# Windowed linear attention on one core: stores moved to ScalarE, halves of q and k stored twice and held in two buffers, masks of the scores in another order

## The chip, the core and the metric

The kernel runs on one core of a Trainium2 chip. A core has TensorE (PE in the profile; its weight loads are PEld), VectorE (DVE), ScalarE (ACT), GpSimd (POOL) and SyncE (SP), each with its own instruction queue that is worked off in order. Transfers (DMAs) are issued by an instruction on one of these queues and then run on 16 shared DMA engines. The metric is the device time of one execution in microseconds (us); the time of a version is the median of its runs.

## The reference

The input x is 4 x 256 x 48 x 48 in float32. Four layers each add to x a function of its group norm (32 groups): a 7 x 7 dilated convolution whose softmax weighs 49 shifted copies, a 3 x 3 convolution of signs, a 3 x 3 convolution with ternary weights, and the layer that the change touches, layer 3:

```python
q = sigmoid(einsum('bchw,oc->bohw', x, Wq)).reshape(b * 8, 32, 48, 48)   # k likewise
v = einsum('bchw,oc->bohw', x, Wv).reshape(b * 8, 32, 48, 48)
v = v / maximum(norm(v, axis=1), 1e-12)
Ik, Ikv = integral(k), integral(einsum('bfhw,bghw->bfghw', k, v))
for w in (1, 2, 4):
    ws = 48 // w
    wk, wkv = box(Ik, ws), box(Ikv, ws)          # sums over a ws x ws window, cut at the edges
    attn = einsum('bdhw,bdfhw->bfhw', q, wkv)
    norm = einsum('bdhw,bdhw->bhw', q, wk)
    outs.append(attn / (norm[:, None] + 1e-6))
x = x + einsum('bchw,oc->bohw', concatenate(outs, axis=1), Wout) + bout
```

`integral` and `box` are cumulative sums in both directions and their four-corner differences with edge padding, so a window of half width h (24, 12, 6) reaches the positions -h to h - 1 around a query as far as the image goes.

## The kernel before, in words

Layers 0 to 2 come first and are not changed. Layer 3 does not form the box sums of k v; it computes scores between keys and queries, masks them by each window, and multiplies them with v.

**Tiling.** The 48 x 48 positions are cut in 6 row blocks of 8 rows (`RB`); a row block has 384 positions (`NB`). A key tile is 8 rows by 16 columns, 128 positions, so there are 18 per image. The 8 heads are taken 4 at a time, which are the 128 channels of one channel block (`ct` or `mo`, 2 of them). A block of work (`Block`) is one batch, one channel block and one row block of queries: 48 blocks. A block meets the key tiles that its widest window sees, so the stream has 720 steps in all, each a pair of block and key tile.

**A step.** `scores` (called by `score`) multiplies, for a pair of heads (`pr` 0 or 1), a key tile with the queries into one of the two PSUM buffers `s`. Keys and queries are in float32r, split in a rounded half `hi` and a remainder `lo`; the contraction of 128 is four groups of 32, keys (hi, lo, hi, lo) against queries (hi, hi, lo, lo). `masked` (called by `cut`) then cuts the scores out of PSUM into a tile `sm`: where the key tile's rows lie wholly in the widest window, only the strips at its column edges are masked by VectorE (`widest`); the middle window is masked by VectorE (`middle`) or, in tiles two row blocks away, copied plainly by ScalarE (`copy`); a narrower window is masked by GpSimd from the middle one. Elsewhere VectorE masks the whole tile. Two steps later (`LAG`) `sums` multiplies `sm` with v into the accumulators `acc0` to `acc2`; what lies wholly in the widest window comes as one product of q with a summed state (`whole`). At a block's end the accumulators are copied to `stage`.

**Order of the work.** The program is written out by hand in one order, and every engine is kept to it: the helper `InOrder` (L149) records each instruction, which is why nearly every row of the profile carries L149 and tiles must tell the rows apart. In each turn of the main loop: fetch the keys of four steps on (`EARLY`), the scores and masks of the second pair of heads, the scores and masks of the next step's first pair, the sums of two steps ago, then one call of `advance`.

**Background.** `advance` lets a list of generators take one step each, as far as they are due; `yield n` means "again in n steps". `take` waits until a buffer counted in `free` is free, `bank` until the shared PSUM bank is, `wait_for` until something is in `made`; `until` turns `advance` inside the main loop until something is made. The generators are:
- `Projection` for the next batch: `load` of x, `qk` (a matmul into `proj_ps`, `sg` by sigmoid, for keys `kt` in the tiles' order, stores to `q_d`, `k_d`, `kf_d`, then `hi` by ScalarE, `lo` by GpSimd, and their stores to `kst_d` and `qst_d`) and `v`;
- `k_sums`: running sums of k (`cs`, a scan on VectorE), column sums of the three windows (`pt`, VectorE, then row by row on GpSimd), stored to `kb_d`;
- `norms`: loads `nhi`, `nlo`, `nq`, multiplies differences of `kb_d` with q on GpSimd, sums over channels on TensorE (`norm_ps`), stores `ns` to `n_d`, loads `nr`, takes its reciprocal, stores `r_d`;
- `state` and `window_state`: sums of k v for `whole`;
- `prepare` and `finish`: load the first channel block's result (`o`) and the norms (`rc`), divide, multiply with Wout (`out_ps`), add x (`res`), store the output.

Each key projection stores its halves in 8 DMAs (two halves, four heads of 32 partitions), each query projection in 8 likewise. `keys` has 7 slots (`KEYS`); a key tile is loaded into the slot whose content is needed latest, by two DMAs of 64 partitions, and a block's queries by four DMAs for each pair of heads. `hi`, `lo` and `pt` have one buffer each: the next writer waits until their stores have landed. In layer 3 all DMAs but two loads of constants are issued on SP's queue. Eight completion semaphores serve the DMAs of the hardware queues in turn, and each DMA waits for the one that used its semaphore before, eight issues back.

## Time and profile before

| | |
|---|---|
| time, 3 runs | 3889.24 us median (3881.86, 3889.24, 3891.01) |
| the profiled execution's own time | 3874.22 us |
| its span | 3872.4 us |
| TensorE matmuls | 3073.5 us, 79% of the span |
| VectorE | 2419.6 us, 62% |
| GpSimd | 1756.2 us, 45% |
| ScalarE | 723.8 us, 19% |
| mean granted TensorE clock | 0.911 |
| DMA | 624.08 MB; q1, which nearly all use, 53.3% of 16 engines |

The page gives the busy time of each engine, the span in 40 slices, the DMA queues, the chain that ended last, the costliest groups of instructions, and the DMA issues. A group is named by line, engine, operation and tiles (out<-in); `keys<-kst_d` is a load of `keys` from `kst_d`, `kst_d<-hi` a store of `hi`. The figures behind it are busy time, the mean of one instruction in ns, and the idle time just before such instructions with what ended most of it. "PE s <- DVE sm" among the waits says that TensorE's writes of `s` waited for VectorE's writes of `sm`, with the total in us, how often, and the longest. Instructions that issue DMAs are not counted as busy. The page's chain that ended last covers only a sliver of this span, so stretches and waits carry the reading here. Layer 3's scores run from 1431 us to the end; the projections that feed its first batch run before, beside the end of layer 2.

### The profile page before, as it was taken

What the parts mean: (1) busy time and instruction counts of PE and PEld (TensorE: products, weight loads), DVE (VectorE), ACT (ScalarE), POOL (GpSimd) and SP (SyncE); (2) the same over time, 40 slices, a digit from 0 to 9 for tenths busy, and PEclk for the clock granted to TensorE, in tenths of its full rate; (3) what the DMA queues carried; (4) which work ended last, traced back from release to release, by engine and by line L of the source; (5) the groups of instructions that cost most, each with busy time, mean ns of one, the idle gap of its engine ahead of it and who ended that gap; (6) DMA issues with size and microseconds to landing.
All of it is one profiled execution on the core that took longest, in us unless ns stands there. A gap on an engine that the chain in (4) does not pass through costs nothing. (4 is left out here: it accounts for less than half of the span.)

```text
span 3872.4 us, 70429 instructions
## 1 busy us (share of the span) xinstructions
PE 3073.5 (79%) x25874; PEld 2092.5 (54%) x25874; DVE 2419.6 (62%) x4987; ACT 723.8 (19%) x1652; POOL 1756.2 (45%) x2644
## 2 busy tenths in 40 slices
PE   3689998998996676577778767778877768989888
PEld 2567677777774464344445444445545445555554
DVE  7876685685653365566656556666556756667665
ACT  0012111111115322222111222211122211111110
POOL 0000210210201145667776567766667767665553
PEclk9799999999998888888889988889988889999999
DMA  7745233234235354566666557666756656754553
GB/s 247 239 134 179 79 122 114 85 120 124 79 100 160 113 145 148 169 196 186 181 176 200 175 177 208 195 185 188 205 166 192 202 161 199 198 149 137 164 145 106
DMA packets 529705, 624.08 MB, mean 161 GB/s; under 512 B 162867, under 2 KB 411475, under 8 KB 528339
## 3 DMA queue, kind: packets, MB, share of 16 engines
q1 hardware_dynamic: 528163, 617.79, 53.3%
q8 instruction: 209, 3.42, 0.4%
q0 software_dynamic: 144, 0.99, 0.1%
q14 instruction: 133, 1.09, 0.1%
q10 hardware_dynamic: 1056, 0.79, 0.1%
HBM read 451.32 MB, written 169.00 MB: 160 GB/s over the span
## 5 line engine op out<-in xcount | busy, mean ns | idle before, releaser
L149 DVE TENSOR_TENSOR sm<-s,masks 128x128 f32<-128x128 f32 (+8 forms) x2592 | 1129.6, 495 | 743.3 <-ACT sm L149 298.1
L149 POOL TENSOR_TENSOR sm<-sm,masks 128x432 f32<-128x432 f32 (+14 forms) x1152 | 825.0, 730 | 751.1 <-DVE sm L149 607.4
L149 PE MATMUL s<-qst,keys 128*128 128x320 f32 (+3 forms) x2880 | 781.2, 379 | 362.1 <-DVE sm L149 200.2
L149 PEld LDWEIGHTS s<-qst,keys 128*128 128x128 f32 x2880 | 477.8, 202 | 639.1 <-issue 310.2
L149 PE MATMUL acc<-sm,vs 128*32 128x64 f32 (+13 forms) x14976 | 697.7, 317 | 7.3 <-POOL sm L149 7.3
L149 PE MATMUL cv<-vx,wt 128*128 128x288 f32 x2080 | 559.1, 425 | 92.8 <-DVE vx L149 51.0
L149 PEld LDWEIGHTS cv<-vx,wt 128*128 128x128 f32 x2080 | 402.3, 198 | 213.4 <-issue 56.4
L149 PEld LDWEIGHTS acc<-sm,vs 128*32 128x32 f32 x14976 | 359.3, 114 | 256.6 <-issue 179.6
L149 ACT COPY sm<-s 128x234 f32<-128x234 f32 (+5 forms) x384 | 131.1, 341 | 1076.7 <-PE s L149 882.7
L149 POOL MEMSET v<- 128x16 f32 (+1 forms) x120 | 18.5, 215 | 684.0 <-DVE vx L149 629.3
L149 PE MATMUL cv<-v,wl 128*128 128x384 f32 x1152 | 228.4, 358 | 29.4 <-DVE x L149 10.8
L149 PEld LDWEIGHTS cv<-v,wl 128*128 128x128 f32 x1152 | 217.2, 197 | 40.9 <-issue 19.5
L149 DVE TENSOR_TENSOR pt<-cs 128x384 f32<-128x384 f32 x144 | 112.7, 784 | 150.1 <-DMA kb_d<-pt 140.6
L149 POOL TENSOR_TENSOR pt<-pt 128x144 f32<-128x144 f32 x336 | 182.9, 544 | 27.7 <-DVE pt L149 5.6
L149 POOL TENSOR_TENSOR v<-l2v,v 128x384 fp32r<-128x384 f32 x96 | 108.4, 1158 | 102.9 <-ACT v L149 93.9
L149 POOL TENSOR_TENSOR nhi<-nhi,nq 128x384 f32<-128x384 f32 x144 | 148.8, 1061 | 0.0
L149 PE MATMUL cv<-pad,wl 128*128 128x384 bf16 x864 | 143.1, 328 | 0.0
L149 PE MATMUL proj_ps<-wv_sb,xn 128*128 128x256 f32 x288 | 91.9, 450 | 59.8 <-ACT sg L149 40.5
L149 PE MATMUL out_ps<-o,wout_sb 128*128 128x384 f32 x288 | 126.3, 521 | 12.7 <-POOL o L149 7.6
L149 PE MATMUL proj_ps<-xn,wk_sb 128*128 128x384 f32 x192 | 89.2, 594 | 52.4 <-ACT vt L149 19.5
L149 PE MATMUL out_ps<-stage,wout_sb 128*128 128x384 f32 x288 | 120.0, 499 | 0.7 <-DVE stage L149 0.7
L149 PEld LDWEIGHTS <-wl 128*128 128x128 bf16 x864 | 83.8, 97 | 59.2 <-issue 0.6
(178 smaller groups left out, 3508.4 us busy)
## 6 DMA issues: line engine op xcount, KB each, us to landing
keys<-kst_d SPq DMA_DIRECT2D x960, 128.0 KB
wt<-wt SPq DMA_DIRECT2D x48, 768.0 KB
qst<-qst_d SPq DMA_DIRECT2D x384, 96.0 KB
kb_d<-pt SPq DMA_DIRECT2D x48, 576.0 KB
rc<-r_d SPq DMA_DIRECT2D x192, 144.0 KB
nhi<-kb_d SPq DMA_DIRECT2D x120, 192.0 KB
nlo<-kb_d SPq DMA_DIRECT2D x88, 192.0 KB
o_d<-stage SPq DMA_DIRECT2D x24, 576.0 KB
```

What stands on the lines that cost most here:

```text
L149: return lambda *args, **kwargs: self.tc.keep_in_program_order(op(*args, **kwargs))
```

## The change

- `kst_d` and `qst_d` hold each half twice, in the order of the contraction: a dimension of 4 in place of 2. A key tile is then loaded by one DMA of 128 partitions in place of two of 64, and a pair's queries by one in place of four.
- The halves are stored by DMAs from all 128 partitions: 12 for a key projection (four copies, three key tiles) in place of 8, and 4 for a query projection in place of 8.
- These stores, and those of `k_d`, `q_d`, `kf_d`, `n_d` and `o_d`, are issued on ScalarE's queue in place of SP's.
- `hi` and `lo` have two buffers in place of one, and they and `pt` are counted as free only 6 steps after their stores (`STORED`). What depends on them is marked as made before this hold.
- `KEYS` is 6 in place of 7, and a slot whose key tile the present step still uses is not taken (`used`, `idle`).
- `norms` issues all loads of `nhi` and `nq` for both channel blocks at once, and loads `nlo` piecewise, one window at a time, in two buffers, with a step after each piece.
- In `masked`, `middle` and `widest` come before `copy`.
- In the main loop the masks of the next step's first pair stand after `advance` in place of before the sums; their scores stay where they were.

```diff
--- before.py
+++ after.py
@@ -81,9 +81,10 @@
 NKT = NRB * NKC
 
 LAG = 2
-KEYS = 7
+KEYS = 6
 EARLY = 4
 QST = 4
+NLO = 2
 ATTN_EPS = 1e-6
 
 
@@ -226,11 +227,11 @@
     k_d = [dram.tile([C, HW], F32, tag=f"k{b}", name=f"k_d{b}") for b in range(B)]
     v_d = [dram.tile([P, NKT, HEADS, D], F32, tag=f"v{b}", name=f"v_d{b}") for b in range(B)]
     kst_d = [
-        dram.tile([NCT, NKT, 2, D, HEADS // NCT, P], F32, tag=f"kst{b}", name=f"kst_d{b}")
+        dram.tile([NCT, NKT, 4, D, HEADS // NCT, P], F32, tag=f"kst{b}", name=f"kst_d{b}")
         for b in range(B)
     ]
     qst_d = [
-        dram.tile([NCT, NRB, 2, D, HEADS // NCT, NB], F32, tag=f"qst{b}", name=f"qst_d{b}")
+        dram.tile([NCT, NRB, 4, D, HEADS // NCT, NB], F32, tag=f"qst{b}", name=f"qst_d{b}")
         for b in range(B)
     ]
     kf_d = [dram.tile([C, HW], F32, tag=f"kf{b}", name=f"kf_d{b}") for b in range(B)]
@@ -280,9 +281,10 @@
         bank_free = step + steps
 
 
-    free = {"xr": 2, "xn": 2, "kt": 2, "sq": 2, "vt": 1, "hl": 1, "ku": 1, "pt": 1, "cs": 1, "o": 1, "rc": 2, "res": 2}
+    free = {"xr": 2, "xn": 2, "kt": 2, "sq": 2, "vt": 1, "hl": 2, "ku": 1, "pt": 1, "cs": 1, "o": 1, "rc": 2, "res": 2}
 
     FETCH = 4
+    STORED = 6
 
     def take(what):
         while free[what] == 0:
@@ -379,30 +381,31 @@
                 act.copy(kt.rearrange("p (c r x) -> p c r x", c=NKC, x=KC), rows)
             yield 1
             if name == "k":
-                sync.dma_start(out=k_d[b][chans, cols], in_=kt)
-            sync.dma_start(out=(q_d if name == "q" else kf_d)[b][chans, cols], in_=t)
+                act.dma_start(out=k_d[b][chans, cols], in_=kt)
+            act.dma_start(out=(q_d if name == "q" else kf_d)[b][chans, cols], in_=t)
             yield from take("hl")
-            hi, lo = (self.scr.tile([P, NB], F32R, tag=x, name=x, bufs=1) for x in ("hi", "lo"))
+            hi, lo = (self.scr.tile([P, NB], F32R, tag=x, name=x) for x in ("hi", "lo"))
             whole = t if name == "q" else kt
             act.copy(hi, whole)
             yield 1
             pool.tensor_sub(lo, whole, hi.bitcast(F32))
             yield 2
-            for half, part in enumerate((hi, lo)):
-                for g in range(HEADS // NCT):
-                    src = part[g * D : (g + 1) * D].bitcast(F32)
-                    if name == "q":
-                        sync.dma_start(out=qst_d[b][mo, a, half, :, g, :], in_=src)
-                    else:
-                        sync.dma_start(
-                            out=kst_d[b][mo, a * NKC : (a + 1) * NKC, half, :, g, :].rearrange(
-                                "c d n -> d c n"
-                            ),
-                            in_=src.rearrange("p (c n) -> p c n", n=P),
+            for n in range(4):
+                if name == "q":
+                    act.dma_start(
+                        out=qst_d[b][mo, a, n].rearrange("d g n -> g d n"),
+                        in_=(hi, lo)[n // 2].bitcast(F32),
+                    )
+                else:
+                    for c in range(NKC):
+                        act.dma_start(
+                            out=kst_d[b][mo, a * NKC + c, n].rearrange("d g n -> g d n"),
+                            in_=(hi, lo)[n % 2][:, c * P : (c + 1) * P].bitcast(F32),
                         )
-            free["hl"] += 1
             free["kt"] += 1
             made.add((name, b, mo, a))
+            yield STORED
+            free["hl"] += 1
 
         def v(self, g, a, c):
             b = self.b
@@ -1607,8 +1610,9 @@
                 out=kb_d[b][:, chans, a * RB : (a + 1) * RB, :].rearrange("w p r x -> p w (r x)"),
                 in_=pt.rearrange("p w r x -> p w (r x)"),
             )
+            made.add(("kb", b, mo, a))
+            yield STORED
             free["pt"] += 1
-            made.add(("kb", b, mo, a))
 
         def norms(b, rb):
 
@@ -1618,7 +1622,6 @@
             def load(ct):
                 chans = slice(ct * P, (ct + 1) * P)
                 hi = scr.tile([P, NW, RB, W], F32, tag="nhi", name="nhi")
-                lo = scr.tile([P, NW, RB, W], F32, tag="nlo", name="nlo", bufs=1)
                 qf = scr.tile([P, RB, W], F32, tag="nq", name="nq")
                 sync.dma_start(
                     out=qf.rearrange("p r w -> p (r w)"),
@@ -1637,31 +1640,41 @@
                             out=hi[:, wi, n:RB],
                             in_=kb_d[b][wi, chans, H - 1 : H, :].to_broadcast([P, RB - n, W]),
                         )
-
-                    y0 = rb * RB - h - 1
-                    n = min(RB, max(0, -y0))
-                    if n < RB:
-                        sync.dma_start(
-                            out=lo[:, wi, n:RB], in_=kb_d[b][wi, chans, y0 + n : y0 + RB, :]
-                        )
-                return hi, lo, qf
+                return hi, qf
+
+            def load_lo(ct, wi):
+                y0 = rb * RB - HALVES[wi] - 1
+                n = min(RB, max(0, -y0))
+                if n == RB:
+                    return None, n
+                lo = scr.tile([P, RB, W], F32, tag="nlo", name="nlo", bufs=NLO)
+                sync.dma_start(
+                    out=lo[:, n:RB],
+                    in_=kb_d[b][wi, ct * P : (ct + 1) * P, y0 + n : y0 + RB, :],
+                )
+                return lo, n
 
             last = min(rb + HALVES[0] // RB, NRB - 1)
             yield from wait_for(
                 *((what, b, ct, at) for what, at in (("kb", last), ("q", rb)) for ct in range(NCT))
             )
-            for ct in range(NCT):
-                hi, lo, qf = load(ct)
-                yield FETCH
-                for wi, h in enumerate(HALVES):
-                    n = min(RB, max(0, h + 1 - rb * RB))
-                    if n < RB:
-                        pool.tensor_sub(hi[:, wi, n:RB], hi[:, wi, n:RB], lo[:, wi, n:RB])
+            loaded = [load(ct) for ct in range(NCT)]
+            pieces = [(ct, wi) for ct in range(NCT) for wi in reversed(range(NW))]
+            los = [load_lo(*pieces[n]) for n in range(NLO)]
+            yield FETCH
+            for at, (ct, wi) in enumerate(pieces):
+                hi, qf = loaded[ct]
+                lo, n = los.pop(0)
+                if lo is not None:
+                    pool.tensor_sub(hi[:, wi, n:RB], hi[:, wi, n:RB], lo[:, n:RB])
+                    if at + NLO < len(pieces):
+                        yield 1
+                if at + NLO < len(pieces):
+                    los.append(load_lo(*pieces[at + NLO]))
+                pool.tensor_mul(hi[:, wi], hi[:, wi], qf)
                 yield 1
-                for wi in range(NW):
-                    pool.tensor_mul(hi[:, wi], hi[:, wi], qf)
-                sums.append(hi)
-                yield 1
+                if wi == 0:
+                    sums.append(hi)
             yield 1
             yield from bank(1)
             ps = ps_m.tile([P, 512], F32, tag="st", name="norm_ps")
@@ -1679,7 +1692,7 @@
             act.copy(ns, ps[0 : D * NW, 0:NB])
             yield 1
             for wi in range(NW):
-                sync.dma_start(out=n_d[b][rb, :, wi, :], in_=ns[D * wi : D * wi + HEADS])
+                act.dma_start(out=n_d[b][rb, :, wi, :], in_=ns[D * wi : D * wi + HEADS])
             nn = HEADS * NW * NB // P
             nr = scr.tile([P, nn], F32, tag="nr", name="nr")
             flat = [d[b][rb].rearrange("h w n -> (h w n)") for d in (n_d, r_d)]
@@ -1765,11 +1778,12 @@
             stacks = []
             for pr in range(NPR):
                 st = qp.tile([P, 2, RB, W], F32, tag="qst", name="qst", bufs=QST)
-                for n in range(4):
-                    sync.dma_start(
-                        out=st[n * D : (n + 1) * D].rearrange("p j r w -> p j (r w)"),
-                        in_=qst_d[b][ct, rb, n // 2, :, 2 * pr : 2 * pr + 2, :],
-                    )
+                sync.dma_start(
+                    out=st.rearrange("p j r w -> p j (r w)"),
+                    in_=qst_d[b][ct, rb, :, :, 2 * pr : 2 * pr + 2, :].rearrange(
+                        "t d j n -> (t d) j n"
+                    ),
+                )
                 stacks.append(st.bitcast(F32R))
             return qs, stacks
 
@@ -1902,9 +1916,9 @@
 
 
 
-                copy(s, tiles)
                 middle(s, tiles)
                 widest(s, tiles)
+                copy(s, tiles)
 
                 wi = NW - 1 if many else 1
                 if wi in wis:
@@ -2009,7 +2023,7 @@
             b, ct, rb = order[i]
             yield 1
             if ct == 0:
-                sync.dma_start(out=o_d[b][rb], in_=stage.rearrange("p w n -> p (w n)"))
+                act.dma_start(out=o_d[b][rb], in_=stage.rearrange("p w n -> p (w n)"))
                 made.add(("done", i))
                 return
             while i not in prepared:
@@ -2121,7 +2135,7 @@
         for n, (i, a, c, _, _) in enumerate(stream):
             uses.setdefault((*order[i][:2], a, c), []).append(n)
         keys = [wts.tile([P, HG, P], F32, name=f"keys{i}") for i in range(KEYS)]
-        held = [None] * KEYS
+        held, used = [None] * KEYS, [-1] * KEYS
 
         def next_use(tile_, n):
             return next((u for u in uses[tile_] if u >= n), len(stream)) if tile_ else len(stream) + 1
@@ -2135,23 +2149,23 @@
             want = (b, ct, a, c)
             if want in held:
                 return
-            at = max(range(KEYS), key=lambda at: next_use(held[at], now))
+            idle = [at for at in range(KEYS) if used[at] < now]
+            at = max(idle, key=lambda at: next_use(held[at], now))
             assert next_use(held[at], now) > n
             until(("k", b, ct, a))
             held[at] = want
-            for half in range(2):
-                sync.dma_start(
-                    out=keys[at][half * 2 * D : (half + 1) * 2 * D],
-                    in_=kst_d[b][ct, a * NKC + c].rearrange("t d g n -> (t d) g n"),
-                )
+            sync.dma_start(
+                out=keys[at], in_=kst_d[b][ct, a * NKC + c].rearrange("t d g n -> (t d) g n")
+            )
 
         def score(n, pr):
 
             i, a, c, at, _ = stream[n]
             if pr == 0 and at == 0:
                 begun(i)
-            ks = keys[held.index((*order[i][:2], a, c))].bitcast(F32R)
-            return blocks[i].scores(pr, a, c, ks)
+            slot = held.index((*order[i][:2], a, c))
+            used[slot] = n
+            return blocks[i].scores(pr, a, c, keys[slot].bitcast(F32R))
 
         blocks, ahead = {}, []
         start(window_state(0))
@@ -2170,8 +2184,7 @@
                 fetch_keys(n + EARLY, n)
                 s1 = score(n, 1)
                 ahead[-1].append(cut(n, s1))
-                if n + 1 < len(stream):
-                    ahead.append([cut(n + 1, score(n + 1, 0))])
+                s0 = score(n + 1, 0) if n + 1 < len(stream) else None
                 i, a, c, at, last = stream[n]
                 if at == 5:
                     midway(i)
@@ -2191,6 +2204,8 @@
                 if last:
                     done(i)
             advance()
+            if n + 1 < len(stream):
+                ahead.append([cut(n + 1, s0)])
         while active:
             advance()
```

## The prediction

> **What bounds the kernel now.** I read the page's first parts, then busy time by stretch, the waits by engine, one stall in the timeline, and the issue times by tile. Nearly every row carries L149, the recording helper, so all goes by tiles. The change touches layer 3 and the projections that feed it, so I cut the span where the fourth stored block of each batch ends: 1431 us is the first score, 2132, 2777, 3390 and 3847 end batches 0 to 3. The busy time of each engine in these stretches (columns: stretch, its length, PE, PEld, DVE, ACT, POOL busy with counts, granted clock, DMA share, GB/s):
>
> ```profile
> 1431.00:2132.00 701.00, 510.56 (x5079) 312.88 (x5079) 422.29 (x875) 130.51 (x330) 472.61 (x710) 0.86 0.62 180
> 2132.00:2777.00 645.00, 493.11 (x5089) 302.68 (x5089) 386.57 (x820) 125.15 (x309) 437.83 (x626) 0.90 0.65 191
> 2777.00:3390.00 613.00, 490.03 (x5065) 302.45 (x5064) 380.43 (x813) 123.85 (x308) 412.53 (x600) 0.91 0.64 186
> 3390.00:3847.00 457.00, 403.48 (x4787) 245.57 (x4787) 296.98 (x671) 58.10 (x170) 251.94 (x382) 0.97 0.48 142
> ```
>
> TensorE is the bound, with holes: it idles 190, 152 and 123 us in batches 0 to 2 and 54 us in batch 3, which has no projection beside it. So 466 of 519 idle us lie where the background runs. Who it waits for there, and what ScalarE and VectorE wait for (waits of layer 3, three answers):
>
> ```profile
> PE s L149 <- DVE sm L149: 200.2, 196, 10.4
> PE s L149 <- DMA keys<-kst_d: 104.7, 27, 15.4
> ...
> PE proj_ps L149 <- ACT vt L149: 39.3, 15, 13.5
> PE proj_ps L149 <- ACT sg L149: 27.8, 14, 8.0
> ...
> ACT hi L149 <- DMA qst_d<-hi: 172.9, 22, 17.4
> ...
> ACT hi L149 <- DMA kst_d<-hi: 139.2, 20, 21.1
> ...
> DVE sm L149 <- ACT sm L149: 298.1, 216, 8.4
> ...
> DVE pt L149 <- DMA kb_d<-pt: 140.6, 28, 10.8
> ```
>
> ScalarE stands 312 us in 42 waits before it may overwrite `hi`, VectorE 141 us before it may overwrite `pt`: each has one buffer that a store still reads. In the timeline of one such stall (start, duration; idle before in brackets) both hold TensorE at once:
>
> ```profile
> 2308.06 2.46 SPq L149 DMA_DIRECT2D kst_d<-hi  x4
> 2310.57 1.84 SPq L149 DMA_DIRECT2D kst_d<-lo  x4
> 2310.97 0.74 DVE L149 TENSOR_TENSOR pt<-cs 128x384 f32<-128x384 f32 x1 [4.30 <-DMA kb_d<-pt]
> ...
> 2311.86 0.51 ACT L149 CAST hi<-kt 128x384 fp32r<-128x384 f32 x1 [10.24 <-DMA kst_d<-hi]
> ...
> 2312.70 1.91 PE L149 MATMUL proj_ps<-wv_sb,xn 128*128 128x256 f32 x4 [4.30 <-ACT vt L149]
> ```
>
> The stores sit on SP's queue, which is nearly full. Its issue times by tile (min/median/max ns):
>
> ```profile
> L149 SPq DMA_DIRECT2D keys<-kst_d x960: 444/592/1959, 1431.6 to 3826.5; - x192
> ...
> L149 SPq DMA_DIRECT2D kst_d<-hi x192: 302/435/1527, 1165.3 to 3139.8; - x192
> ...
> L149 SPq DMA_DIRECT2D qst<-qst_d x384: 302/420/1677, 1416.4 to 3787.5; - x192
> ```
>
> Summed over the trace, SP issues for 1536 us of the 2416 (569 of it keys) and waits for much of the rest.
>
> Following each idle stretch of TensorE over 0.25 us back through its releasers, as the page's chain does from the end, sorts the idle time by root. Layer 3: stores of the halves 122 us, `pt` store 75, key and `rc` loads 92, VectorE's own queue 90, ScalarE's own 42; the rest hops and small pieces. The early stretch (1120 to 1431): halves 39.
>
> **The change part by part.**
>
> *Halves in two buffers, held six steps.* ScalarE's and POOL's waits on `hi`/`lo` go, since a buffer is asked for again only some 20 us after its stores are issued, and a `kst_d<-hi` store lands 2.4 us after issue (median of the trace's completions). It can give at most 122 + 39 = 161 us, at least the 90 of the stalls longest in it; I take **-150**.
>
> *`pt` held six steps.* A store of `pt` lands in 3.5 us. At most -75, at least -40; I take **-70**.
>
> *SP relieved.* Built, the program has 536 key loads of 256 KB (960 of 128; six slots instead of seven cost 56 reloads), 96 `qst` loads (384), and 1008 stores now on ScalarE. In layer 3 SP's issue time falls by 569 - 536 x 0.6 = 247, by 171 - 96 x 0.6 = 113, and by 363 for the moved stores: 1536 to about 813 us. Key and `rc` waits are 92 us; but every transfer, on either queue, still waits for the one eight issues before it, so a key load can now stand behind a store on ScalarE. From 0 to -80; I take half, **-45**.
>
> *Strips ahead of copies.* The scores' PSUM buffer is free when strips and copy are both done; before, VectorE waits for the copy (298 us in 216 waits), now the copy waits for the strips. The same two operations in a row, so TensorE sees little: +20 to -40, **-10**.
>
> *ScalarE issues the stores.* In layer 3 it gets 36 k projections x 14, 36 q x 5, 72 norms and 24 `o_d`: 780 issues. The two loads it issues today take 484 and 556 ns, SP's rows for these stores 430 to 503: 780 x 0.48 = 374 us on its in-order queue, beside 437 busy. Queued behind them: copies of scores, evacuations of `proj_ps`, `stage`. What matters is clumps. Two buffers let both halves of a channel block come together: 24 k stores in a row, 18 times, 11.5 us each by the issue price; 8 q stores, 4 us. TensorE can go on for about two tiles, 2 x 2.77 us (1494 us busy over 540 tiles), before it needs ScalarE. So q clumps cost nothing, k clumps 18 x (11.5 - 5.5) = 108. If landing sets the pace, at eight in flight, the slowest row (`rc<-r_d`, 5.6 us) gives 24 / 8 x 5.6 = 17 us and 207. Lower end 50, should issuing overlap computing. I take 12.5 us, near the issue rows: **+126**.
>
> The new stores have an outer dimension of 4. In this trace `n_d<-ns`, outer dimension 8, completes with 9 updates of its semaphore, every other transfer with 16. [...]
>
> *Later background.* Counting the planner's own steps: the first block begins at step 113, not 89, because each projection now takes 4.5 steps instead of 3; the remainder lands between layer 2 and the first tile. About five projections, 2 us each: **+10** (0 to 25). In batch 0 the norms come late and the main loop turns without a tile: 64 steps in all instead of 28. One POOL operation a step, 1.06 us (`nhi`): 36 x 1.1 = **+40** (0 to 70).
>
> *Background between the pairs' masks.* It now stands ahead of the mask that frees the buffer TensorE asks for next, not behind it. About 96 scans of 1.07 us, 144 `pt` of 0.78 and the chains of `vr` (2.9 us, 18 times) push it back by a few tenths each: **+25** (-20 to +80).
>
> *Bytes.* Stores of halves double and keys are reloaded: 14 + 14 + 14 = 42 MB on some 430 in layer 3, at a DMA share of 0.61. Hidden unless the share saturates: **+5** (0 to 60).
>
> Sum: -150 - 70 - 45 - 10 + 126 + 10 + 40 + 25 + 5 = -69. The clock follows idleness (0.86 at 27% idle, 0.97 at 12%; the scores cost 205 us in batch 0, 184 in batch 3): scores and sums together are 97 us dearer over the 466 idle us of batches 0 to 2, so another 0.2 x 69 = -14. The profiled execution took 3874.2 us (span 3872.4), 15 under the median of 3889.2. 3874 - 83 = 3791, and 3806 as a median; I say **3805**.
>
> **Rivals.**
>
> 1. *ScalarE's queue becomes the stall* (slower). The k clumps take 17 us and hold the shared completion slots, so key loads gain nothing and q clumps (18) cost 3 us each: -150 - 70 - 0 - 10 + 207 + 54 + 10 + 40 + 25 + 30 = +136, with the clock +163: about **4050**; a clump of 16 us with 40 us of q and keys gives 3980. For it: ScalarE's queue was hurt by 42 waits of 7.4 us, and 18 of 17 us are as much. Against it: 2.4 us landings. With the other terms as taken, it decides from clumps of 16.3 us (126 + 69 = 195 = 18 x 10.8).
> 2. *The stalls really vanish.* Batches 0 to 2 come near the last one's rate: each would be 457 + (498 - 403) = 552 us, 653 today, so 303 us is the ceiling. Clumps at 50, steps at 15, masks at 0, keys at -80 give -150 - 70 - 80 - 30 + 65 = -265, less a third left as hops: about **3700**. For it: the roots named are the largest waits; against: new work on ScalarE.
> 3. *It changes nothing to speak of*: gains and clumps cancel, within 0.3% (12 us, about what a measurement of this kernel can tell from none): **3889**.
>
> **How the numbers follow.** Forecast (3740 to 3875) 0.37, rival 2 (under 3740) 0.18, rival 1 0.40, since it needs only 4 us more per clump, rival 3 0.05. Faster 0.55, same 0.05, slower 0.40. The range takes the forecast, most of rival 2 and three quarters of rival 1, up to its own price: 3670 to 4050. The forecast's own range is 3740 to 3875.
>
> **What would show it.** Right: no waits of ACT `hi` on DMA; DVE `pt` on `kb_d` near zero; DVE `sm` on ACT `sm` replaced by ACT `sm` on DVE `sm`; SP's issue time near 815 us; idle of batches 0 to 2 under 400 us; ACT rows of 24 `kst_d` stores lasting 11 to 14 us. Wrong: such rows of 16 us or more, TensorE waiting for ScalarE's `sg`, `vt`, `sm` by over 200 us, key waits no smaller, a DMA share over 0.75, or holes in batch 0 of 10 us where the loop turns without tiles.

## The result

The changed kernel takes 4350.32 us (median of 4 runs, 4349.62 to 4352.24); the kernel before took 3886.66 us in the same comparison. The ratio is 1.1194, 95% interval 1.1175 to 1.1213: 464 us slower, where 3805 us was forecast. The profiled execution has a span of 4350.4 us.

The busy time of the engines in the stretches of layer 3, cut at the same places of the work as before (columns as there: stretch, length, PE, PEld, DVE, ACT, POOL, granted clock, DMA share, GB/s):

```profile
1501.00:2324.00 823.00, 536.27 (x5074) 323.71 (x5074) 413.19 (x852) 139.19 (x348) 438.62 (x653) 0.81 0.54 166
2324.00:3148.00 824.00, 542.33 (x5127) 324.17 (x5128) 406.64 (x842) 122.45 (x297) 452.26 (x663) 0.82 0.53 164
3148.00:3862.00 714.00, 506.84 (x5022) 306.13 (x5022) 376.38 (x808) 123.58 (x306) 411.09 (x600) 0.86 0.59 182
3862.00:4326.00 464.00, 410.42 (x4805) 246.65 (x4803) 301.13 (x673) 59.10 (x172) 272.20 (x403) 0.97 0.51 158
```

Batches 0 to 2 lost 122, 179 and 101 us, batch 3, without a projection beside it, 7; the first score starts 65 us later, after the stretch in which the first projections run (1501.4 for 1436.2 us; the first stretch of before begins at 1431, 5 us ahead of its first score). TensorE's idle time in batches 0 to 2 went from 465 to 776 us, and the same matmuls kept it busy for 92 us more, at a granted clock of 0.81 to 0.86 for 0.86 to 0.91. The DMA share of these batches fell to 0.53 to 0.59, from 0.62 to 0.65: the DMA engines as a whole are not the limit here.

The waits of layer 3 (three answers: TensorE's, VectorE's, and those of SP's queue before it issues):

```profile
PE s L150 <- DMA keys<-kst_d: 215.7, 35, 30.2
PE proj_ps L150 <- ACT sg L150: 214.0, 31, 20.7
PE s L150 <- ACT sm L150: 149.8, 87, 10.6
PE proj_ps L150 <- ACT vt L150: 53.0, 17, 12.4
PE s L150 <- DVE sm L150: 47.6, 78, 4.7
...
DVE pt L150 <- DMA kb_d<-pt: 6.8, 1, 6.8
...
SPq L150 <- DMA n_d<-ns: 204.7, 30, 25.3
```

One more row of before, and two of e4, a kernel below that has the change without its stores, which are as before and on SP (TensorE's waits in each):

```profile
PE s L149 <- ACT sm L149: 7.6, 1, 7.6
```

```profile
PE s L150 <- DMA keys<-kst_d: 241.5, 63, 26.0
PE s L150 <- ACT sm L150: 80.4, 81, 4.4
```

`pt` waits almost no more, as forecast. But TensorE's waits for ScalarE's `sg` and `vt` at `proj_ps` went from 67 to 267 us. Those for `sm` went from 8 to 150, but some 80 of them stand in e4 too and none in e8, which is e4 with the old order: with the strips ahead of the copies the copy is what comes last, and the waits for VectorE's `sm` fell from 200 to 48. The waits for keys doubled (105 to 216 us); e4, with no store on ScalarE, has 242. One stall in the timeline shows keys and ScalarE at once:

```profile
2836.53 0.44 SPq L150 DMA_DIRECT2D kp<-kf_d  x1
...
2837.32 2.07 ACTq L150 DMA_DIRECT2D kst_d<-hi  x3
...
2842.65 3.46 ACTq L150 DMA_DIRECT2D kst_d<-hi  x3
...
2846.25 3.44 ACTq L150 DMA_DIRECT2D kst_d<-lo  x3
2846.85 15.01 SPq L150 DMA_DIRECT2D rc<-r_d  x8
2849.79 2.41 ACTq L150 DMA_DIRECT2D kst_d<-hi  x3
...
2857.19 2.54 ACTq L150 DMA_DIRECT2D kst_d<-lo  x3
2859.77 0.95 ACT L150 COPY state<-kv_ps 32x96 f32<-32x96 f32 x4 [22.05 <-DMA kst_d<-hi]
2861.95 1.06 SPq L150 DMA_DIRECT2D keys<-kst_d  x2
2866.93 0.87 PE L150 MATMUL s<-qst,keys 128*128 128x320 f32 x2 [21.26 <-DMA keys<-kst_d]
```

A clump, 24 stores in a row, holds ScalarE's queue from 2837.3 to 2859.7 us, 22.4 us. Beside it SP needs 15 us to issue eight `rc` loads, with the key loads behind them. What SP waited for most between 2836 and 2868 us:

```profile
SPq L150 <- DMA kst_d<-lo: 9.4, 5, 4.2
SPq L150 <- DMA kst_d<-hi: 7.5, 5, 3.0
```

So the stores hold up both queues, through the eight completion semaphores that both share. Counted from the trace's semaphore updates, no transfer of either queue in layer 3 begins before the one that used its semaphore last has landed. Of SP's 1553 (from 1431 us on), 144 begin within 0.2 us after a transfer of ScalarE's landed; in this stall an `rc` load begins at 2856.29 us, and the store with its semaphore landed at 2856.27. It is landing that sets the pace of the clump, not issuing: 24 issues at 0.54 to 0.62 us are 13 to 15 us. In these 22.4 us 24 stores and 9 loads of SP pass through eight semaphores, each used about four times, and a store lands 5.5 us after its issue begins (median of the 24): an estimate of 33 / 8 x 5.5 = 22.7 us. The rows of the stores themselves:

```profile
L150 ACTq DMA_DIRECT2D kst_d<-hi x288: 512/542/2133, 1161.7 to 3648.7; - x144
L150 ACTq DMA_DIRECT2D kst_d<-lo x288: 513/622/2415, 1164.0 to 3651.4; - x144
...
L150 ACTq DMA_DIRECT2D qst_d<-hi x96: 518/529/3477, 1178.9 to 3584.1; - x96
L150 ACTq DMA_DIRECT2D qst_d<-lo x96: 512/682/4100, 1180.1 to 3590.2; - x96
```

By the same count, in layer 3 a store of `kst_d` now completes with 5 updates and lands 4.8 us after its issue begins (median; before 16 updates, 2.4 us for `hi` and 1.7 for `lo`), one of `qst_d` 7.8 us (`hi`) and 10.5 us (`lo`) after (before 2.1 and 1.6). The rows of halves' stores with nothing else on ScalarE between them, each from its first issue to the end of its last, add up to 787 us over the trace.

### The profile page after: what moved, and what is told of

It reads as the page before. It is cut to its first block, busy times and chain, and to the rows that moved or that the text cites. A ratio compares the mean times of both kernels' runs of the same rounds, so it can differ in the third digit from the quotient of the medians.

```text
span 4350.4 us, 69346 instructions
## 1 busy us (share of the span) xinstructions
PE 3196.1 (73%) x25874; PEld 2152.9 (49%) x25874; DVE 2427.7 (56%) x4987; ACT 730.1 (17%) x1654; POOL 1752.8 (40%) x2644
## 5 line engine op out<-in xcount | busy, mean ns | idle before, releaser
L150 DVE TENSOR_TENSOR sm<-s,masks 128x128 f32<-128x128 f32 (+8 forms) x2592 | 1150.2, 495 | 1177.8 <-PE s L150 720.6
L150 PE MATMUL s<-qst,keys 128*128 128x320 f32 (+3 forms) x2880 | 835.0, 395 | 497.9 <-DMA keys<-kst_d 215.7
L150 PEld LDWEIGHTS s<-qst,keys 128*128 128x128 f32 x2880 | 496.8, 209 | 801.9 <-issue 393.0
L150 PE MATMUL acc<-sm,vs 128*32 128x64 f32 (+13 forms) x14976 | 715.3, 322 | 9.6 <-POOL sm L150 9.4
L150 PEld LDWEIGHTS cv<-v,wl 128*128 128x128 f32 x1152 | 223.8, 203 | 50.8 <-issue 22.4
L150 PE MATMUL proj_ps<-xn,wq_sb 128*128 128x384 f32 x192 | 105.2, 686 | 187.0 <-ACT sg L150 158.1
L150 PE MATMUL proj_ps<-xn,wk_sb 128*128 128x384 f32 x192 | 101.7, 666 | 91.8 <-ACT sg L150 59.2
L150 PEld LDWEIGHTS proj_ps<-xn,wq_sb 128*128 128x128 f32 x192 | 44.8, 257 | 222.1 <-ACT sg L150 164.8
L150 ACT COPY stage<-acc 128x384 f32<-128x384 f32 x144 | 63.9, 483 | 414.4 <-PE acc L150 397.2
```

The costliest lines, as they stand in the source:

```text
L150: return lambda *args, **kwargs: self.tc.keep_in_program_order(op(*args, **kwargs))
```

## The experiments

Two theories for the stores stood at the start. A: their form (128 partitions at once, outer dimension 4) makes them land late. B: ScalarE's in-order queue is held by issuing. The ratios are to the kernel before, measured beside each.

**e1: the halves' stores back on SP.**

```diff
-                    act.dma_start(
+                    sync.dma_start(
                         out=qst_d[b][mo, a, n].rearrange("d g n -> g d n"),
...
-                        act.dma_start(
+                        sync.dma_start(
                             out=kst_d[b][mo, a * NKC + c, n].rearrange("d g n -> g d n"),
```

> The changed kernel with the stores of the halves (12 for a key, 4 for a query projection, from 128 partitions each) issued on SP's queue again; k_d, kf_d, q_d, n_d, o_d stay on ScalarE. Theory A (the form of these stores: they complete with 5 updates of their semaphore where the others show 16, and land in 4.8 us for kst_d and 7.8 to 10.6 us for qst_d, so with eight in flight a clump of 24 takes 22 us): the clump now holds SP's queue and the completion slots, ScalarE is free but key loads wait behind the stores; 4050 to 4350 us. Theory B (ScalarE's in-order queue: 780 issues there, whatever their form): the stall is gone, 3800 to 3950 us.

4120.36 us, ratio 1.0606 (1.0578 to 1.0634): 230 us under the changed kernel, 234 over the one before. That lies in A's range, but neither theory holds alone: moving the stores away from ScalarE gives back half.

**e2: another layout, so that each store writes 128 even rows.**

```diff
-        dram.tile([NCT, NKT, 4, D, HEADS // NCT, P], F32, tag=f"kst{b}", name=f"kst_d{b}")
+        dram.tile([NCT, NKT, 4, HEADS // NCT, D, P], F32, tag=f"kst{b}", name=f"kst_d{b}")
...
-                            out=kst_d[b][mo, a * NKC + c, n].rearrange("d g n -> g d n"),
+                            out=kst_d[b][mo, a * NKC + c, n].rearrange("g d n -> (g d) n"),
...
-            sync.dma_start(
-                out=keys[at], in_=kst_d[b][ct, a * NKC + c].rearrange("t d g n -> (t d) g n")
-            )
+            for t in range(4):
+                sync.dma_start(
+                    out=keys[at][t * D : (t + 1) * D],
+                    in_=kst_d[b][ct, a * NKC + c, t].rearrange("g d n -> d g n"),
+                )
```

(and `qst_d` and its loads likewise)

> The changed kernel with kst_d and qst_d laid out with the heads ahead of the 32 channels, so that each store writes 128 even rows; same number, bytes and queue of stores as in the changed kernel. For this a key tile is loaded by four DMAs of 32 partitions, not one, and a pair's queries by four, on SP (some 1900 issues more, at about 0.35 us; SP had room for them). Theory A (form): the stores complete with 16 updates and land in 2 to 3 us, clumps of 24 last 12 to 14 us in place of 22, time 3800 to 4000 us. Theory B (count of issues on ScalarE): as the changed kernel or slower, 4300 to 4450 us.

4257.53 us, ratio 1.0964 (1.0941 to 1.0986): outside both ranges. Of the form, A was right: 16 updates, landing in 2.0 to 2.5 us, 489 us of ScalarE in rows of stores in place of 787. The time did not follow, most likely because the key loads in four pieces brought a stall of their own: TensorE waited 367 us for keys (216 in the changed kernel), and batch 3, which has no stores beside it, took 512 us from its first score to its last (468 in the changed kernel). The edit mixed two things; e15 and e18 separate the form better.

**e3: the kernel before with the wide form, each half once, on SP.**

```diff
-            for half, part in enumerate((hi, lo)):
-                for g in range(HEADS // NCT):
...
+                    for c in range(NKC):
+                        sync.dma_start(
+                            out=kst_d[b][mo, a * NKC + c, half].rearrange("d g n -> g d n"),
+                            in_=part[:, c * P : (c + 1) * P].bitcast(F32),
+                        )
```

> The kernel before, with nothing changed but the form of the halves' stores: from all 128 partitions as in the change, but each half once, on SP, 6 in place of 8 for a key projection and 2 in place of 8 for a query projection. Theory A (form): the one buffer of hi and lo is held some 3 us longer for each of 48 key projections and 6 to 8 us longer for 48 query projections, of which TensorE sees about half: 3980 to 4150 us, with waits of ScalarE for hi of over 500 us where the kernel before has 312. Theory B (queue): fewer issues and no load on ScalarE, 3850 to 3900 us.

3950.49 us, ratio 1.0168 (1.0139 to 1.0196). The form alone costs 64 us, with fewer stores: again 5 updates, landing in 3.6 to 4.1 us (`kst_d`) and 5.2 to 7.2 us (`qst_d`), and ScalarE's waits for `hi` are 484 us over the trace, 371 in the kernel before. A holds in kind, at less than its price.

**e4: the changed kernel with the stores, layout and loads of before, all on SP.** What stays is the rest of the change.

```diff
-                act.dma_start(out=k_d[b][chans, cols], in_=kt)
-            act.dma_start(out=(q_d if name == "q" else kf_d)[b][chans, cols], in_=t)
+                sync.dma_start(out=k_d[b][chans, cols], in_=kt)
+            sync.dma_start(out=(q_d if name == "q" else kf_d)[b][chans, cols], in_=t)
...
+            for half, part in enumerate((hi, lo)):
+                for g in range(HEADS // NCT):
```

> The changed kernel with the stores of before: layout, form, count, and all on SP, and the loads of before; what stays is two buffers of the halves, the holds of six steps, six key slots, norms in pieces, strips ahead of copies, and the background between the pairs' masks. By the terms of the prediction for these (-150 - 70 - 10 + 10 + 40 + 25, with the clock -30): about 3700 us. Rival: the gains come back as key loads behind a fuller SP queue, or the rest (later start, steps without a tile, masks behind the background) costs more than taken: 3890 us or above.

3943.4 us, ratio 1.0154 (1.0131 to 1.0177). The rest of the change, forecast at about -155, is 57 us slower than before. Each idle stretch of TensorE in layer 3, followed back to its root as in the prediction, shows where it went (how far such a walk follows a late load is a choice that shifts a root by some tens of us): halves and `pt` went from some 200 us to nearly nothing, but keys and `rc` from about 100 to over 200 (TensorE's waits for keys are the 242 us above), GpSimd from some 15 to over 40. The stalls named did vanish; the idle time from the first score to the last did not (514 and 534 us). The same matmuls also kept TensorE busy longer there, 1945 us in place of 1891, at a granted clock of 0.89 for 0.90 (the profiled execution of before is 12 us quicker than its median); what else makes them dearer is open. The first score comes at 1428 us, not later than before, so the changed kernel's late start comes with its stores.

**e5: the changed kernel with its four copies stored head by head, on ScalarE.**

```diff
+                for g in range(HEADS // NCT):
...
+                        act.dma_start(
+                            out=kst_d[b][mo, a * NKC : (a + 1) * NKC, n, :, g, :].rearrange(
+                                "c d n -> d c n"
+                            ),
```

> The changed kernel with its four copies of the halves stored head by head, from 32 partitions each as before the change: 16 stores in place of 12 for a key projection and 16 in place of 4 for a query projection, all still on ScalarE; the single loads of keys and queries stay. Form says: 16 updates, landing in 2 us, a clump is now 32 issues at 0.45 to 0.5 us, about 15 us in place of 22, and no wait of 8 to 13 us between query stores; 4080 to 4220 us. Count of issues on ScalarE says: a third more for keys and four times as many for queries, 4400 to 4550 us.

4421.95 us, ratio 1.1379 (1.1333 to 1.1424). One issue is shorter and the updates are 16, but there are twice as many stores, and the rows of them hold ScalarE for 947 us:

```profile
L150 ACTq DMA_DIRECT2D kst_d<-hi x384: 309/440/1709, 1166.7 to 3728.4; - x192
...
L150 ACTq DMA_DIRECT2D qst_d<-hi x384: 308/432/1592, 1184.0 to 3678.4; - x192
```

B is right here: with the other form the rows hold the queue 160 us longer than the 787 of the changed kernel, and the time is 72 us longer.

**e7, e8, e9: the slots and the masks.** e7 is the kernel before with `KEYS = 6`. e8 is e4 with the order of the masks of before, e9 is e4 with `KEYS = 7` and `NLO = 1`.

```diff
-                middle(s, tiles)
-                widest(s, tiles)
                 copy(s, tiles)
+                middle(s, tiles)
+                widest(s, tiles)
...
-                s0 = score(n + 1, 0) if n + 1 < len(stream) else None
+                if n + 1 < len(stream):
+                    ahead.append([cut(n + 1, score(n + 1, 0))])
```

> The kernel before with 6 key slots in place of 7 and nothing else. If the slots are what the kernel with the old stores lost (its waits of TensorE for keys were 242 us where before has 105 in layer 3, and its key loads 1062 in place of 960): 3920 to 3950 us with those waits near 200. If not: the reloads alone, 3885 to 3905 us.

> The kernel with the old stores (two buffers, holds, six slots, norms in pieces), with the masks' order of before: copies ahead of strips, and the next pair's masks ahead of the sums and the background. If the order of the masks cost the gain: 3850 to 3900 us. If it does nothing: 3930 to 3950 us.

> The kernel with the old stores and the new order of masks, with 7 key slots; to make room nlo has one buffer in place of two. If the slots cost the gain: 3860 to 3900 us, with waits of TensorE for keys near 105 us in layer 3. If they do nothing: 3930 to 3960 us.

e7: 3911.39 us, ratio 1.007 (1.0042 to 1.0098); e8: 3939.66 us, 1.0142 (1.0095 to 1.019); e9: 3923.45 us, 1.0094 (1.0064 to 1.0125). The seventh slot is worth about 27 us in the kernel before, a little over the range for the reloads alone; TensorE's waits for keys are 112 us in e7 and 223 in e9, so the slots are not what raised them in e4. Against e4's 1.0154, the order of the masks and the place of the background, taken back together, are worth nothing that shows.

**e10 and e15: the kernel before with its halves' stores on ScalarE, in the old form (e10) and in the wide form (e15).**

```diff
-                        sync.dma_start(out=qst_d[b][mo, a, half, :, g, :], in_=src)
+                        act.dma_start(out=qst_d[b][mo, a, half, :, g, :], in_=src)
```

> The kernel before with one edit: its stores of the halves (8 for each projection, from 32 partitions, landing in 1.6 to 2.4 us) are issued on ScalarE's queue in place of SP's. If ScalarE's in-order queue is what makes the changed kernel slow: 576 issues of 0.45 us in layer 3, 260 us, of which the kernels with the halves on ScalarE and on SP (4350 and 4120 for some 700 us of issuing) suggest that a third shows: 3950 to 4000 us. If the number of issues is harmless and only the wide form and the doubling hurt: 3860 to 3900 us.

> The kernel before with the halves' stores from 128 partitions each (as in e3, once each, 6 for a key and 2 for a query projection) and issued on ScalarE (as in e10). The two alone measured 64 and 39 us over before. If they only add: 3970 to 4000 us. If late landings hurt more on ScalarE, because they hold its queue: 4030 to 4100 us. If half the issues of e10 make ScalarE's part small: 3940 to 3960 us.

e10: 3921.85 us, ratio 1.0107 (1.0077 to 1.0137). The same 768 stores in number as in the changed kernel, but at most eight in a row, landing in 2.2 to 2.8 us: 39 us, between the two ranges. e15: 4020.67 us, 1.0354 (1.0324 to 1.0385), between the range for a plain sum and that for more. With e3 the four corners are 1 (old form, SP), 1.0168 (wide, SP), 1.0107 (old, ScalarE) and 1.0354: 31 us over the sum. Late landings and ScalarE's queue make each other worse.

**e14: the clump spread.**

```diff
                             in_=(hi, lo)[n % 2][:, c * P : (c + 1) * P].bitcast(F32),
                         )
+                yield 1
```

> The changed kernel with a step of the background after every copy of the halves, so that a key projection issues three stores and a query projection one in a step, in place of 12 and 4 in a row. Same form, number and queue. If the clumps are what costs (24 stores in a row hold ScalarE's queue for some 22 us, TensorE can go on for 5.5): 4100 to 4220 us. If the total of the issuing (some 700 us) or the late landing costs wherever it stands: 4300 to 4400 us.

4232.39 us, ratio 1.0893 (1.0869 to 1.0917): 118 us under the changed kernel, a little over the range for clumps. The rows in sum are as long (782 us). So about a quarter of the loss goes with the stores in a row, and more remains. The rows are not all gone: 14 of 12 stores or more stand in the trace, 26 in the changed kernel, and landings are as late (4.8 us for `kst_d`).

**e16 and e18: all stores of the changed kernel on SP, in the wide form (e16) and head by head (e18).** The edits are those of e1 and e5, with `k_d`, `q_d`, `kf_d`, `n_d` and `o_d` on SP as in e4.

> The changed kernel with all stores on SP, their form and doubling kept; against e1 only k_d, q_d, kf_d, n_d and o_d come back from ScalarE. In e1 SP stood 123 us before loads that wait for n_d, in the changed kernel 205, in before 35. If that cross-queue wait costs: 4040 to 4090 us. If the small stores are harmless on ScalarE: 4100 to 4140 us.

> The changed kernel with all stores on SP (as e16) and the four copies of the halves stored head by head from 32 partitions, 16 stores for each projection; single loads of keys and queries stay. If the wide form is what e16 loses to the old stores: 3950 to 3990 us, landings near 2 us. If the doubling is (bytes and 1536 stores on SP): 4050 to 4150 us.

e16: 4067.34 us, ratio 1.0474 (1.0454 to 1.0494). Against e1, the small stores on ScalarE cost 53 us. SP stands 205 us before loads that wait for `n_d<-ns` in the changed kernel, 123 in e1, 63 in e16 and 35 in the kernel before. TensorE's waits for `sg` and `vt` at `proj_ps` rise as well, from 24 us in e16 to 74 in e1, so which of the two is the 53 us is not shown. Its waits for keys go the other way: 348 us in e16, 302 in e1, 216 in the changed kernel. e18: 4011.56 us, 1.0315 (1.0284 to 1.0347), between the ranges: of the 124 us from e4 to e16, 68 come from storing each half twice (with single loads; twice the stores as well as the bytes), 56 from the wide form.

The runs now make a ladder from the kernel before to the changed one, in ratios: 1.0154 without any change of the stores (e4), 1.0315 with four copies and single loads (e18), 1.0474 in the wide form (e16), 1.0606 with the small stores on ScalarE (e1), 1.1194 with the halves' stores there too. In points: 1.5, 1.6, 1.6, 1.3 and 5.9.

**e11, e12, e17: parts of the rest alone, in the kernel before.** e11 has the new `norms`. e12 has only the hold of `pt`. e17 has only the two buffers of the halves, held six steps, and one buffer of `xr` in place of two to make room.

```diff
-            free["pt"] += 1
             made.add(("kb", b, mo, a))
+            yield STORED
+            free["pt"] += 1
```

> The kernel before with the norms of the changed kernel (all loads of nhi and nq first, nlo in pieces with a step after each), nothing else. The prediction's terms for later norms and for steps without a tile say up to +40, 3900 to 3930 us, with TensorE waiting for nhi at norm_ps; if the norms are harmless: 3870 to 3895 us.

> The kernel before with the hold of pt alone (six steps after its store, what depends on it marked as made before the hold). The prediction's term: -40 to -75, 3810 to 3850 us. The rival, that the time comes back as another wait since the later of several chains decides: 3865 to 3895 us. VectorE's waits for kb_d<-pt go to near nothing in both.

> The kernel before with hi and lo in two buffers, held six steps after their stores; pt, norms, slots, masks and stores as before. To make room xr has one buffer in place of two. The prediction's term: 3735 us (-150). By subtracting from the kernel with old stores (+57) what the hold of pt (+64), norms in pieces (+61) and six slots (+27) measured alone: -95, 3790 us. Rival: the stall only moves to other waits, 3870 to 3900 us.

e11: 3943.77 us, ratio 1.0155 (1.0126 to 1.0184), above both ranges. e12: 3946.8 us, 1.0168 (1.0131 to 1.0205), also above both. e17: 3856.65 us, 0.9935 (0.9912 to 0.9957), better than its rival's range and the only kernel here that beats the one before, by 26 us. The waits of e12 (VectorE's and TensorE's, over the trace):

```profile
DVE pt L149 <- DMA kb_d<-pt: 6.8, 1, 6.8
...
PE s L149 <- DMA keys<-kst_d: 140.5, 40, 12.4
```

VectorE's 141 us of waits are gone, and the kernel is 64 us slower. The background came later: the last store of batch 0's `kb_d` is at 1903 us in place of 1707, that of batch 1's last `r_d`, which ends its norms, 541 us after the batch's first score in place of 397. Between the first scores of the batches stand 670, 682 and 653 us, before 686, 644 and 615: batch 0 got shorter, and 1 and 2 lost more. Roots at halves rose from 122 to 163 us, at keys and `rc` from 89 to 129.

The waits of e17, likewise:

```profile
PE s L149 <- DVE sm L149: 215.3, 191, 14.1
PE s L149 <- DMA keys<-kst_d: 153.3, 51, 19.4
PE proj_ps L149 <- ACT sg L149: 29.7, 18, 7.7
...
DVE pt L149 <- DMA kb_d<-pt: 180.9, 29, 17.4
...
ACT hi L149 <- DMA qst_d<-hi: 7.1, 1, 7.1
ACT hi L149 <- DMA kst_d<-hi: 5.2, 2, 3.2
```

371 us of ScalarE's waits for `hi` over the trace are 12. In the roots of TensorE's idle time, halves went from 161 us (with the early stretch) to under 50. But VectorE's waits for `pt` rose from 141 to 181 us and TensorE's for keys from 105 to 153, and the roots at both rose by 25 us or more.

**e13 and e19: what became late next.** e13 is e9 with the eight `rc` loads spread over steps; e19 is e17 with a second buffer of `pt`, six buffers of `sm` for seven and the new place of the background.

```diff
                         .partition_broadcast(D),
                     )
+                    if g % 2:
+                        yield 1
```

```diff
-        tc.tile_pool(name="smp", bufs=2 * (LAG + 1) + 1, reuse_waits="tile") as smp,
+        tc.tile_pool(name="smp", bufs=2 * (LAG + 1), reuse_waits="tile") as smp,
...
-            pt = scr.tile([P, NW, RB, W], F32, tag="pt", name="pt", bufs=1)
+            pt = scr.tile([P, NW, RB, W], F32, tag="pt", name="pt")
```

> The kernel with the old stores and seven slots, and one more edit: in prepare, a step of the background after every second rc load, so that its eight broadcasts (5.6 us each) no longer go out in a row ahead of key loads. If rc loads ahead of key loads are where the gain of the buffers went: 3860 to 3890 us, with the idle time rooted in rc loads down from 38 us to 10. If the wait only moves: 3910 to 3930 us.

> The kernel of e17 (two buffers of the halves, held) with two buffers of pt and no hold of it. To make room the pool of sm has 6 buffers in place of 7, and the next pair's masks stand after the background as in the change. If the pt stall is worth what the walk says (106 us rooted in it, of which e17 showed a sixth for the halves): 3820 to 3845 us. If it moves to the keys: 3850 to 3880 us. If six sm buffers hold VectorE up: above 3880 us.

e13: 3956.24 us, ratio 1.0193 (1.0165 to 1.0221), slower than e9 and above both ranges: TensorE's waits for keys stay (223 us in both). Spreading the loads in this way is not the cure. e19: 3908.11 us, 1.0058 (1.0036 to 1.0079), in the range given for six `sm` buffers that hold VectorE up. Its stretches by batch, then those of e17:

```profile
1424.00:2072.00 648.00, 506.13 (x5031) 304.64 (x5031) 433.75 (x862) 137.65 (x339) 477.22 (x710) 0.89 0.67 196
...
3347.00:3891.00 544.00, 444.38 (x4808) 255.93 (x4809) 309.27 (x683) 59.28 (x173) 260.83 (x390) 0.94 0.42 123
```

```profile
1425.00:2092.00 667.00, 508.49 (x5032) 312.37 (x5033) 424.02 (x862) 137.19 (x340) 474.17 (x710) 0.86 0.65 189
...
3369.00:3823.00 454.00, 405.73 (x4806) 246.58 (x4805) 299.84 (x681) 59.72 (x173) 260.72 (x391) 0.98 0.50 148
```

Batch 0 is 19 us shorter, batches 1 and 2 differ by 3 and 1, and batch 3, which makes no `pt`, takes 90 more. Of the edits that act in that batch, the `sm` buffer taken away is the likeliest, since the new order and place of the masks together cost e4 nothing against e8; it was not tried alone, and neither was the second `pt` buffer with seven `sm` buffers. Whether the second `pt` buffer is worth something stays open.

## Why the prediction was wrong

The sum was -83 us and the change measured +464, 547 apart. Two runs split this. The parts other than the stores, -155 in the sum, measured +57 (e4): 212 of it. The stores, with the bytes and the relief of SP +86 in the sum, measured +407 (from e4 to the changed kernel): 321 of it. The rest is the term for the clock. So two steps failed: idle time rooted in a wait was taken as what the wait is worth, and a row of stores on ScalarE was priced by issuing where landing sets its length.

**Halves in two buffers, -150.** The waits went as forecast, the time did not: alone, -26 us (e17). The step that failed was to take the idle time rooted in a wait as its worth. `pt` and keys were nearly as late, and their waits grew when this one went.

**`pt` held, -70.** Wrong in sign: +64 alone (e12). I wrote of the wait removed and not of the one added: a hold of six steps keeps the only buffer some 20 us more (2405 us for 720 steps are 3.3 us each), so the chain of `k_sums`, and the norms behind it, run later into the next batches. That the later place is what costs is argued from the stretches, not shown by a run of its own.

**SP relieved, -45.** SP's issue time fell, from 1533 to 677 us in layer 3, but TensorE's waits for keys rose from 105 to 216 us. The text named a reason, that a key load can stand behind a store on ScalarE since eight completions are shared, and the stall above shows one that does. It is not what raised the sum: the waits are 242 us in e4, with no store on ScalarE and SP as full as before, and 348 in e16, and the stores on ScalarE bring them down. The other parts of the change raised them; the halves' buffers alone to 153 (e17), the hold of `pt` alone to 140 (e12). What makes the rest is open, and no run has the relief of SP alone.

**ScalarE issues the stores, +126.** The mechanism was named and mis-sized. It measured +230 for the halves (e1) and +53 for the small stores (e16), for which I had only their issue time; that SP's loads of what they write stand in order behind them may be part of the 53, beside ScalarE's own time. The step that failed is the length of a clump: of the two paces that I weighed, issuing (11.5 us) and landing at eight in flight (17 us), I took 12.5 us, near the issue rows, and the 2.4 us landings held against rival 1 were those of the old form. Landing set it: 22.4 us in the stall above, 19 to 27 us in all 8 unbroken rows of 24. The loads of SP in the same slots, for which neither pace had a term, make the rest. The number of clumps was wrong the other way: 8 rows of 24 in place of 18, beside 18 rows of 12 that last 9.9 us (median). That stores in a row cost something as such is shown by e14 (-118).

**The form of the stores.** The sum had no term for it; the one sign before was `n_d<-ns`, outer dimension 8, with 9 updates. Every store of the halves in the changed kernel, outer dimension 4, shows five, and in layer 3 those of `kst_d` land 4.8 us after their issue begins. No run shows the clump of 16 us from which rival 1 has its 3980 us; the 8 unbroken rows of 24 show 19 to 27 us. A store into the same layout with the 32 channels outermost on both sides was not tried.

**Later background, +10 and +40.** The norms alone measured +61 (e11). **Bytes, +5.** The doubling measured 68 us with the old form (e18 to e4); the runs don't part the bytes from the number of stores. **Six slots,** counted only as reloads: +27 (e7). **Strips ahead of copies -10, background between the masks +25.** Nothing to be seen of the two together (e8).

**The clock, -14.** Its direction followed the idleness as written: TensorE's busy time grew by 123 us over the trace (3073.5 to 3196.1) with the same number of matmuls, a quarter of the loss. In batches 0 to 2 it is 92 us for 310 more of idleness, 0.3 for each, where I took 0.2.

**The rivals.** Rival 1, the slower one, was the right one in its mechanism, that the clumps hold the shared completion slots, at 4050 us for 4350: it had the clump at 17 us and kept the gains of -220, which in e4 are none. Of the signs given for a wrong forecast, rows of 24 stores above 16 us, TensorE's waits for ScalarE over 200 us and key waits no smaller all came true, though the last also comes true without a store on ScalarE (e4).

## What to carry to other kernels

Idle time that a walk roots in one wait is only a ceiling where several chains are about equally late: here over 110 us of removed roots gave 26 us. Before moving stores to a compute engine's queue, count how many come in a row, how long each takes to land, and which loads on another queue wait for them or share their completion slots: here a row of 24 lasted 22.4 us, about as long as the 33 transfers of both queues in it need to land, eight at a time (an estimate of 22.7 us from the 5.5 us of its stores). A hold that lets a planner wait in place of an engine delays everything behind that buffer (the hold of `pt` alone measured +64 us, e12), so its length belongs in the sum.

## What the runs showed of the hardware

A store of the same 64 KB took 4.8 us to land with an outer dimension of 4 (the changed kernel) and about 2 us as 128 even rows (e2), and issuing it took 0.54 to 0.62 us (median) against 0.44. The granted clock fell with the holes: 0.81 in a batch in which TensorE idled 35% of the time, 0.97 where it idled 12%, and in batches 0 to 2 the same matmuls took 92 us more beside 310 us more of idle time, so each us of stall cost about 0.3 of one more.
